# A graph layer on one Trainium2 core: gathering every 44th quad of edge tiles from SyncE instead of GpSimd

## The chip, the cores and the metric

The kernel runs on one core of a Trainium2 chip. A core has TensorE (PE, with its weight loads shown as PEld), VectorE (DVE), ScalarE (ACT), GpSimd (POOL) and SyncE (SP), which run side by side and wait for each other through semaphores, and 16 DMA engines that the queues of SP, ACT and POOL share. The metric is the device time of the whole program in microseconds (us), the median of several runs.

## What is computed

It is one equivariant graph layer with a residual and a layer norm. There are 12,500 nodes of 160 numbers (64 scalars, 32 vectors of three), and 400,000 edges, sorted by destination. Cut to what matters:

```
h     = linear(x) * a                           # per node: 64 + 96 numbers
w     = silu(edge_scalars @ fc_w1) @ fc_w2      # per edge: 224 weights
e     = h[edge_src]                             # the gather: 160 numbers per edge
m     = products of w, e and edge_attr          # per edge
agg   = segment_sum(m, edge_dst)                # per node
o     = linear(agg) + self_connection(x)
out   = layernorm(x + gated(o))
```

The row of `h` that an edge needs is given by `src`, which is random, so it has to be fetched by an index.

## The kernel before, in words

First the table `h_tab` (12,500 rows of 160 floats, 640 bytes each) is computed and written to DRAM (L245 to L315), and the destinations are reduced to the first node of every block (`rows`). Then the loop over the edges runs (L755 to L787), and it takes nearly the whole span.

A tile is 128 edges; 3125 tiles are taken four at a time, a quad, so there are 782 steps. Three tiles make a block, and 24 tiles (six steps) a chunk, whose edge scalars `es` are loaded together by two DMAs on SP (L219). The indices `idx` and the edge attributes `eat` are loaded for 60 tiles at a time (L180, L181). `fetch(n + 4)` asks for what the step four ahead needs.

In a step, these things happen:

- `gather` (L429): POOL issues four indirect DMAs, one per tile, which bring 128 rows of `h_tab` each into one of four `hg` buffers (pool `deep`). The gather for step n + 4 has to wait until DVE has done with the buffer in step n.
- `weights` (L438): PE multiplies the hidden layer `hid` with `w2` into `pw` (two PSUM buffers).
- `products` (L449): DVE multiplies `pw` and `hg` into `pr` in four instructions, one at L455 and three at L463. The last of them frees the `hg` buffer. Between them two hooks run, which may call `turn`'s second half (L571) and `add_up` (L727).
- `select_quad` (L495): DVE makes the selection matrix `sel` (L501, L504).
- `sum_up` (L712): PE multiplies `sel` of two steps earlier with `pr` and sums a block in `pa` (L511). A full pair of blocks is copied to SBUF by ACT (L677) and transposed by PE two steps later (L520).
- `hide(n + 2)` (L635): every other step PE and ACT compute the hidden layer (L424, L426) of the step two ahead.
- `output` (L691): once 16 blocks are ready, PE applies the second linear map (L536) and ACT copies the result to `os` (L539). The 16 results are added into `acc` by DVE (L544) at a base that comes from `rows`, two in a step at most, `add_up` handing them out.
- `finish` (L547): as soon as four tiles of nodes are complete, they are turned (PE, L570), gated, normed and stored (the `x` rows loaded at L564, the result stored at L603, both on SP). There are 25 such jobs. The last one has buffers of its own (pool `ends_fin`).

The order on PE, DVE, ACT and POOL in the loop is that of the program text (`manual_schedule`, L749); SP is not in that list there, and its order is chosen by the scheduler. Every DMA signals one of eight semaphores that the hardware queues take in turn (POOL has eight of its own), and an issue waits until the DMA before it on that semaphore has landed. The loop that repeats work for unusually wide blocks (L820 and on) is not entered with these inputs.

The bases of 16 blocks are read in one go in `output`, into 16 registers of DVE:

```
702:  _, values = nc.values_load_multi_w_load_instructions(
703:      rows[0:1, run[0]:run[0] + m], engines=[ENG.DVE], min_val=0, max_val=N - 1,
704:      skip_runtime_bounds_check_because="every entry of dst is the index of a node")
```

Of the kernel before, what the change touches and what calls it, by code (L numbers as in the profile page):

```python
# [10 lines left out]
F32 = mybir.dt.float32  # L11
I32 = mybir.dt.int32
I16 = mybir.dt.int16
BF16 = mybir.dt.bfloat16
# [17 lines left out]
Q = 4  # L32
SB = 4 * BT
SIDE = SB
AHEAD = 5 * SB
NF = 4

MARGIN = 128
NO = 16
# [13 lines left out]
def gnn_kernel(  # L53
# [21 lines left out]
    nc = tc.nc  # L75
    N = x.shape[0]
# [110 lines left out]
    def index(t):  # L187
        a0, idx, _ = ahead(t)
        return idx[:, t - a0:t - a0 + 1]
# [239 lines left out]
    def gather(pool, idx):  # L429
# [5 lines left out]
                in_offset=bass.IndirectOffsetOnAxis(ap=i, axis=0))  # L435
        return hg

    def weights(psum, hid, slots):  # L438

        pw = psum.tile([P, Q, 256], F32, name="pw")  # L440
        n = len(slots)
        for t in sorted(range(n), key=lambda t: (slots[t][1], slots[t][0])):
            half, c = slots[t]
            r = slice(half * S, (half + 1) * S)
            nc.tensor.matmul(pw[:, t, :NWT], hid[r, c * P:(c + 1) * P], w2[r],  # L445
                             start=True, stop=True)
        return pw
# [98 lines left out]

    def finish(fin, psum, t0, nt, p, most=NF):  # L547


        whole = nt if p == P else nt - 1  # L550
        xt = fin.tile([P, most, D], F32, name="xt")
        z = fin.tile([P, most, 2 * V3], F32, name="z")
        sg = fin.tile([P, most, V3], F32, name="sg")
        y = fin.tile([P, most, D], F32, name="y")
        st = fin.tile([P, most, 6], F32, name="st")
        mv = fin.tile([P, most, 2], F32, name="mv")
        rs = fin.tile([P, most], F32, name="rs")
# [8 lines left out]
        def turn(k):  # L566
            c = (t0 + k) * P
# [7 lines left out]
        def gates():  # L575
            nc.scalar.activation(sg[:, :nt], z[:, :nt, :V3], AF.Sigmoid)  # L576

        def gated():
            nc.vector.tensor_mul(y[:, :nt, :S], z[:, :nt, :S], sg[:, :nt, :S])
# [5 lines left out]
        def residual():  # L585
            nc.vector.tensor_add(y[:, :nt], y[:, :nt], xt[:, :nt])  # L586

        def moments():
            for k in range(nt):
# [4 lines left out]
        def root():  # L594
            nc.scalar.activation(rs[:, :nt], mv[:, :nt, 1], AF.Sqrt, bias=eps)  # L595

        def norm():
            nc.vector.reciprocal(rs[:, :nt], rs[:, :nt])
# [15 lines left out]

    with tc.tile_pool(
        name="fin", bufs=1
    ) as fin, tc.tile_pool(name="ends_fin", bufs=1) as ends_fin, tc.tile_pool(
        name="late", bufs=2
    ) as late, tc.tile_pool(name="edge", bufs=2) as edge, tc.tile_pool(
        name="deep", bufs=4  # L620
# [1 line left out]
        name="pa_ps", bufs=2, space=PSUM  # L622
    ) as pa_ps, tc.tile_pool(name="misc_ps", bufs=2, space=PSUM) as misc_ps:
        hids = {}

        def fetch(n):

# [63 lines left out]
        def output(n, blocks):  # L691
            while adds:
                for a in add_up(adds[0][0]):
                    add(*a)
            os = second(late, misc_ps, tts[0], tts[1], len(blocks))
            at_base = {}
            run = sorted(blocks)
            while run:
                m = 1
                while m < len(run) and run[m] == run[0] + m:  # L700
                    m += 1
                _, values = nc.values_load_multi_w_load_instructions(
                    rows[0:1, run[0]:run[0] + m], engines=[ENG.DVE], min_val=0, max_val=N - 1,
                    skip_runtime_bounds_check_because="every entry of dst is the index of a node")
                at_base.update(zip(run[:m], values))
                run = run[m:]
            adds.extend((n + 2, b, os, k, at_base[b]) for k, b in enumerate(blocks))

        assert NB % 2 == 0
        ended = set()  # L710
# [109 lines left out]
        with tc.For_i(0, n_redo, 1):  # L820
# [5 lines left out]
            with tc.For_i(0, n_again, 1) as g, tc.For_i(0, GT, 1) as k:  # L826
# [21 lines left out]
                with tc.For_i(first + W, last + 1, W) as base:  # L848
# [12 lines left out]
            for pool, job, most in [(fin, job, NF) for job in jobs] + [(ends_fin, last_job, LAST)]:  # L861
# [51 lines left out]
```

## Time and profile before

| what | value |
|---|---|
| median of 3 runs | 5161.72 us (5152.41 to 5164.67) |
| the profiled execution's own time | 5152.41 us |
| its span, first to last instruction | 5150.6 us |
| granted TensorE clock, mean | 0.829 |
| gathers on POOL (L433) | 3125, 966 ns each |
| packets of the gather queue | 150,000, 256.2 MB |
| packets of SP's queue | 128,802, 145.95 MB |
| mean DMA rate | 80 GB/s |

The time of a run is that of the program on the device, and the profile shows one such execution. In the views, a group's line gives the engine, the operation, the tiles written and read, the count, the busy time and the mean of one in nanoseconds, then the idle time of the engine just before and what ended most of it. In the waits, the three numbers are the total in us, how many times, and the longest. In the timeline, the first number is the start in us and the second the duration; what stands in brackets is the idle time before it and what ended it. "remote" is a semaphore whose sender the profile could not name; of the instruction at L455 it is PE's semaphore, the only one that instruction itself waits for.

### The profile page before, as it was taken

The page shows a single profiled execution, that of the slowest core. Times are in us where ns is not written, and L with a number is a line of the kernel's source. Part 1 is how long each engine was busy: PE and PEld are TensorE (multiplying, and loading weights), DVE is VectorE, ACT ScalarE, POOL GpSimd, SP SyncE. Part 2 cuts the span into 40 slices and gives each one's busy share as a digit, 9 for nine tenths or more (in the row PEclk, how much of TensorE's full clock was granted, in tenths as well). Part 3 has the DMA queues.
Part 4 walks back from the last instruction along what each step waited for, and adds up shares of the span by engine and source line. Part 5 has one row for each costly group of instructions (what it writes and reads, how often), then busy time and mean ns, then how long its engine had stood idle before and what let it go on. Part 6 is the DMA issues. An engine that isn't in the chain of part 4 may idle for free. (4 is left out here: it accounts for less than half of the span.)

```text
span 5150.6 us, 54423 instructions
## 1 busy us (share of the span) xinstructions
PE 3755.2 (73%) x17408; PEld 1766.8 (34%) x17408; DVE 2432.3 (47%) x6363; ACT 918.4 (18%) x3014; POOL 3040.2 (59%) x3134
## 2 busy tenths in 40 slices
PE   3776777766777777776777777777777777777776
PEld 3333333333333333333333333333333333333333
DVE  3444444544544444444444445444454444544545
ACT  0111111221211111111111122111121111211212
POOL 3665566656656556556566666665665565556554
PEclk7888888888888888887888888888887888888888
DMA  6333333333333333333333333333333333333322
GB/s 188 84 74 72 85 80 73 86 75 78 84 71 83 80 72 79 83 74 77 82 76 80 79 79 85 75 79 78 80 79 78 78 80 78 78 74 85 76 69 53
DMA packets 292619, 414.35 MB, mean 80 GB/s; under 512 B 74900, under 2 KB 239649, under 8 KB 292084
## 3 DMA queue, kind: packets, MB, share of 16 engines
q0 software_dynamic: 150000, 256.20, 20.6%
q1 hardware_dynamic: 128802, 145.95, 12.6%
q10 hardware_dynamic: 13526, 8.64, 0.6%
q8 instruction: 143, 2.34, 0.2%
q14 instruction: 148, 1.21, 0.1%
HBM read 394.54 MB, written 16.01 MB: 80 GB/s over the span
## 5 line engine op out<-in xcount | busy, mean ns | idle before, releaser
L433 POOL DMA_INDIRECT hg<-h_tab,idx x3125 | 3017.5, 966 | 2072.2 <-DVE oh L501 1113.3
L511 PE MATMUL pa<-pr,sel 128*64 128x416 f32 x6250 | 1599.8, 595 | 185.2 <-issue 160.5
L455 DVE TENSOR_TENSOR pr<-pw,hg 128x512 f32<-128x512 f32 x782 | 539.3, 690 | 2451.0 <-remote 1427.1
L445 PE MATMUL pw<-w,hid 64*128 64x224 f32 x6250 | 975.2, 419 | 363.8 <-issue 178.1
L463 DVE TENSOR_TENSOR pr<-pw,hg 128x384 f32<-128x384 f32 x2346 | 1154.0, 548 | 0.0
L445 PEld LDWEIGHTS pw<-w,hid 64*128 64x128 f32 x6250 | 629.0, 210 | 712.7 <-issue 508.3
L511 PEld LDWEIGHTS pa<-pr,sel 128*64 128x64 f32 x6250 | 456.4, 151 | 932.3 <-issue 867.9
L520 PE MATMUL pt<-ident,sa 128*128 128x128 f32 (+1 forms) x2084 | 378.1, 309 | 381.3 <-ACT hid L426 110.7
L677 ACT COPY sa<-pa 128x416 f32<-128x416 f32 x521 | 262.2, 503 | 1755.2 <-remote 706.0
L424 PE MATMUL ph<-es,w 128*128 128x512 f32 (+1 forms) x784 | 474.1, 686 | 54.3 <-ACT t L527 31.0
L520 PEld LDWEIGHTS pt<-ident,sa 128*128 128x128 f32 (+1 forms) x2084 | 238.2, 143 | 758.1 <-issue 392.5
L536 PE MATMUL po<-tt,l 128*96 128x256 f32 (+3 forms) x1360 | 346.8, 405 | 108.6 <-ACT t L527 67.3
L426 ACT ACTIVATE hid<-ph 128x512 f32<-128x512 f32 x392 | 233.7, 596 | 939.7 <-remote 516.8
L504 DVE TENSOR_TENSOR sel<-oh,eas 128x256 f32<-128x256 f32 x782 | 336.3, 430 | 37.5 <-ACT eas L488 0.2
L524 ACT COPY tt<-pt 128x192 f32<-128x192 f32 x521 | 165.3, 317 | 1027.3 <-remote 514.6
L536 PEld LDWEIGHTS po<-tt,l 128*96 128x96 f32 x1360 | 228.6, 178 | 243.0 <-issue 94.6
L424 PEld LDWEIGHTS ph<-es,w 128*128 128x128 f32 x784 | 128.2, 204 | 348.2 <-issue 268.2
L544 DVE TENSOR_TENSOR acc<-acc,os 96x32 f32 x1042 | 194.9, 187 | 26.3 <-ACT os L539 6.9
L501 DVE TENSOR_TENSOR oh<-rel,iota 128x64 f32<-128x64 int16 x782 | 171.4, 219 | 0.0
L570 PE MATMUL pp<-ident,acc 96*128 96x96 f32 x196 | 43.5, 313 | 171.8 <-DVE acc L544 98.0
L526 ACT COPY tt<-pt 128x32 f32<-128x32 f32 x521 | 103.0, 198 | 0.0
L539 ACT COPY os<-po 96x512 f32<-96x512 f32 (+2 forms) x68 | 38.3, 563 | 328.5 <-PE po L536 113.5
(70 smaller groups left out, 795.9 us busy)
## 6 DMA issues: line engine op xcount, KB each, us to landing
es<-in_es_t_dram SPq DMA_DIRECT2D x260, 384.0 KB
hg<-h_tab,idx POOLq DMA_INDIRECT x3125
h_tab<-ht ACTq DMA_DIRECT2D x6, 1280.0 KB
xt<-in_x_dram SPq DMA_DIRECT2D x23, 320.0 KB
out_dram<-y SPq DMA_DIRECT2D x23, 320.0 KB
xv<-in_xv_t_dram SPq DMA_DIRECT2D x25, 187.5 KB
eat<-in_ea_dram SPq DMA_DIRECT2D x30, 120.0 KB
xs<-in_xs_t_dram SPq DMA_DIRECT2D x25, 125.0 KB
```

The costliest lines, as they stand in the source:

```text
L424: nc.tensor.matmul(ph[:k, c], w1[:k, :k], es[:k, t0 * P + c0 * P:t0 * P + c1 * P], start=True, stop=True)
L426: nc.scalar.activation(hid[:k, c], ph[:k, c], AF.Silu, scale=1.0 / math.sqrt(64))
L433: nc.gpsimd.indirect_dma_start(out=hg[:, t, :], out_offset=None, in_=h_tab, in_offset=bass.IndirectOffsetOnAxis(ap=i, axis=0))
L445: nc.tensor.matmul(pw[:, t, :NWT], hid[r, c * P:(c + 1) * P], w2[r], start=True, stop=True)
L455: nc.vector.tensor_mul(two, pw[:, :n, :2 * S].rearrange("p t (k c) -> p t k c", k=2), hg[:, :n, None, :S].to_broadcast([P, n, 2, S]))
L463: nc.vector.tensor_mul(pr[:, :n, first:first + V3].rearrange("p t (i c) -> p t i c", i=3), pw[:, :n, None, 2 * S + k * V:2 * S + (k + 1) * ...
L504: nc.vector.tensor_mul(sel[:, :n], oh[:, :, None, :].to_broadcast([P, n, 4, W]), by_slot(tiles[0][0])[:, u:u + n, :, None].to_broadcast([P ...
L511: nc.tensor.matmul(pa[half * ROWS:(half + 1) * ROWS, :NPR], sel[:, t].rearrange("p k w -> p (k w)"), pr, start=start, stop=stop)
L520: nc.tensor.transpose(pt[:c, four * P:four * P + k], sa[:k, four * P:four * P + c], ident[:k, :k])
L536: nc.tensor.matmul(po[:, k, :nb], l2[:b, terms[to, part, four]], a[:, :nb], start=(n == 0), stop=(n == len(of) - 1))
L544: nc.vector.tensor_add(window, window, os[:, :, b])
L677: nc.scalar.copy(sa, pas.pop(j)[:, :NPR])
```

## The change

There are three edits.

1. Steps 52, 96, ..., 756 (every 44th, 17 in all; the list `own`) are not gathered by POOL. 50 steps ahead of such a step m, SP loads the 512 indices of the quad into `at_bytes` (four DMAs, `places`). 46 steps ahead DVE multiplies them by 640, to byte addresses, and 44 jobs are queued (`rows_of`). One job is issued in each step: SP reads 12 addresses (8 at the end of a tile) into registers and issues one plain DMA of 640 bytes per edge, from `h_tab` at that address to one partition of the buffer `hq` (two buffers). Step m then takes `hq` in the place of `hg`.
2. The last job of nodes uses the pool `fin` of the other jobs, with two buffers for `xt`; the other tiles are allocated when its first tile is turned (`held`). `ends_fin` is gone.
3. The base of a block is no longer read with 15 others in `output`, but alone in `add_up`, just before it is used, with the check of its bounds.

SP is added to the engines whose order in the loop is that of the program.

```diff
+OWN = 44
+BATCH = 12
...
+    own = [n for n in range(OWN + 8, len(steps) - 4, OWN) if len(steps[n][2]) == Q]
+    by_bytes = h_tab.rearrange("n d -> (n d)").bitcast(U8)
+    row_bytes = 4 * D
+    def places(pool, n):
+        at_bytes = pool.tile([Q, P], I32, name="at_bytes")
+        for k, (t, _, _) in enumerate(steps[n][2]):
+            g, u = divmod(t, GT)
+            with nc.allow_non_contiguous_dma(reason="the indices of one tile"):
+                nc.sync.dma_start(at_bytes[k:k + 1],
+                                  src[g][:, u:u + 1].rearrange("p u -> u p"))
+        return at_bytes
+    def rows_of(pool, at_bytes):
+        hq = pool.tile([P, Q, D], F32, name="hq")
+        flat_hq = hq.rearrange("p t d -> p (t d)").bitcast(U8)
+        jobs = []
+        for t, p0 in ((t, p0) for t in range(Q) for p0 in range(0, P, BATCH)):
+            def job(t=t, p0=p0):
+                _, values = nc.values_load_multi_w_load_instructions(
+                    at_bytes[t:t + 1, p0:min(P, p0 + BATCH)], engines=[ENG.SP], min_val=0,
+                    max_val=(N - 1) * row_bytes,
+                    skip_runtime_bounds_check_because="every entry of src is the index of a node")
+                for i, v in enumerate(values):
+                    p = p0 + i
+                    nc.sync.dma_start(flat_hq[p:p + 1, t * row_bytes:(t + 1) * row_bytes],
+                                      by_bytes[ds(v, row_bytes)][None])
+            jobs.append(job)
+        return hq, jobs
...
+        def fetch_rows(n):
+            for m in own:
+                if n == max(1, m - OWN - 6):
+                    at_of[m] = places(mine, m)
+                if n == max(3, m - OWN - 2):
+                    nc.vector.tensor_scalar_mul(at_of[m], at_of[m], float(row_bytes))
+                    hq_of[m], jobs = rows_of(mine, at_of[m])
+                    rows_due.extend((m, job) for job in jobs)
+            for _, job in rows_due[:1]:
+                job()
+            del rows_due[:1]
...
             fetch(n + 4)
-            hg = gather(deep, [index(t) for t, _, _ in tiles])
+            fetch_rows(n)
+            hg = hq_of.pop(n) if n in own else gather(deep, [index(t) for t, _, _ in tiles])
...
-        with tc.manual_schedule(engines={ENG.PE, ENG.DVE, ENG.Activation, ENG.Pool}):
+        with tc.manual_schedule(engines={ENG.PE, ENG.DVE, ENG.Activation, ENG.Pool, ENG.SP}):
...
-            at_base = {}
-            run = sorted(blocks)
-            while run:
...
-                _, values = nc.values_load_multi_w_load_instructions(
-                    rows[0:1, run[0]:run[0] + m], engines=[ENG.DVE], min_val=0, max_val=N - 1,
-                    skip_runtime_bounds_check_because="every entry of dst is the index of a node")
-                at_base.update(zip(run[:m], values))
-                run = run[m:]
-            adds.extend((n + 2, b, os, k, at_base[b]) for k, b in enumerate(blocks))
+            adds.extend((n + 2, b, os, k) for k, b in enumerate(blocks))
...
-            _, b, os, k, base = adds.pop(0)
+            _, b, os, k = adds.pop(0)
+            base = nc.values_load(rows[0:1, b:b + 1], engines=[ENG.DVE], min_val=0, max_val=N - 1)
...
-        xt = fin.tile([P, most, D], F32, name="xt")
+        xt = fin.tile([P, most, D], F32, name="xt", bufs=2)
+        held = []
...
-            last_steps = finish(ends_fin, misc_ps, *last_job, most=LAST)
+            last_steps = finish(fin, misc_ps, *last_job, most=LAST)
```

More of the change, by code (lines that the diff above doesn't have):

```diff
@@ L13 @@
 I16 = mybir.dt.int16
+U8 = mybir.dt.uint8
 BF16 = mybir.dt.bfloat16
@@ L550, in finish @@
         whole = nt if p == P else nt - 1
-        xt = fin.tile([P, most, D], F32, name="xt")
[L552 to L557, printed above, removed]
+        xt = fin.tile([P, most, D], F32, name="xt", bufs=2)
+        held = []
         if whole < nt:
@@ L566, in turn @@
         def turn(k):
+            if not held:
+                held.extend(fin.tile([P, most, *shape], F32, name=name) for name, shape in (
+                    ("z", [2 * V3]), ("sg", [V3]), ("y", [D]), ("st", [6]), ("mv", [2]),
+                    ("rs", [])))
+            z = held[0]
             c = (t0 + k) * P
@@ L575, in gates @@
         def gates():
+            z, sg = held[:2]
             nc.scalar.activation(sg[:, :nt], z[:, :nt, :V3], AF.Sigmoid)
         def gated():
+            z, sg, y = held[:3]
             nc.vector.tensor_mul(y[:, :nt, :S], z[:, :nt, :S], sg[:, :nt, :S])
@@ L585, in residual @@
         def residual():
+            y = held[2]
             nc.vector.tensor_add(y[:, :nt], y[:, :nt], xt[:, :nt])
         def moments():
+            _, _, y, st, mv, _ = held
             for k in range(nt):
@@ L594, in root @@
         def root():
+            mv, rs = held[4:]
             nc.scalar.activation(rs[:, :nt], mv[:, :nt, 1], AF.Sqrt, bias=eps)
         def norm():
+            _, _, y, _, mv, rs = held
             nc.vector.reciprocal(rs[:, :nt], rs[:, :nt])
@@ L616, in gnn_kernel @@
         name="fin", bufs=1
-    ) as fin, tc.tile_pool(name="ends_fin", bufs=1) as ends_fin, tc.tile_pool(
+    ) as fin, tc.tile_pool(
+        name="mine", bufs=2
+    ) as mine, tc.tile_pool(
         name="late", bufs=2
@@ L624, in gnn_kernel @@
         hids = {}
+        at_of, hq_of, rows_due = {}, {}, []
+        def fetch_rows(n):
[9 more added lines that the diff above has]
+            del rows_due[:1]
+            assert all(m > n for m, _ in rows_due)
         def fetch(n):
@@ L695, in output @@
             os = second(late, misc_ps, tts[0], tts[1], len(blocks))
-            at_base = {}
-            run = sorted(blocks)
-            while run:
-                m = 1
-                while m < len(run) and run[m] == run[0] + m:
-                    m += 1
-                _, values = nc.values_load_multi_w_load_instructions(
-                    rows[0:1, run[0]:run[0] + m], engines=[ENG.DVE], min_val=0, max_val=N - 1,
-                    skip_runtime_bounds_check_because="every entry of dst is the index of a node")
-                at_base.update(zip(run[:m], values))
-                run = run[m:]
-            adds.extend((n + 2, b, os, k, at_base[b]) for k, b in enumerate(blocks))
+            adds.extend((n + 2, b, os, k) for k, b in enumerate(blocks))
         assert NB % 2 == 0
@@ L860, in gnn_kernel @@
                     nc.vector.tensor_scalar_add(r, r, -float(W))
-            for pool, job, most in [(fin, job, NF) for job in jobs] + [(ends_fin, last_job, LAST)]:
+            for pool, job, most in [(fin, job, NF) for job in jobs] + [(fin, last_job, LAST)]:
                 job_steps = finish(pool, misc_ps, *job, most=most)
```

## The prediction, written before the result was known

> **What bounds the kernel now.** I read the page first, then the waits of DVE and POOL, then the timeline of those two engines, because the answer of the first two views is misleading here.
>
> ```profile
> PE 3755.2 (73%) x17408; PEld 1766.8 (34%) x17408; DVE 2432.3 (47%) x6363; ACT 918.4 (18%) x3014; POOL 3040.2 (59%) x3134
> ...
> L433 POOL DMA_INDIRECT hg<-h_tab,idx x3125 | 3017.5, 966 | 2072.2 <-DVE oh L501 1113.3
> ...
> L455 DVE TENSOR_TENSOR pr<-pw,hg 128x512 f32<-128x512 f32 x782 | 539.3, 690 | 2451.0 <-remote 1427.1
> ```
>
> No engine is full. POOL spends 966 ns in a gather and then 0.30 us of issue, so one gather per 1.25 us and a quad of four in 5.0 us; a step takes 6.43 us (the start of L455 in all 782 steps). POOL also stands idle 1113 us for a buffer that DVE has to free. The waits of DVE say the same from the other side:
>
> ```profile
> DVE pr L455 <- remote: 1427.1, 165, 14.5
> DVE pr L455 <- PE pw L445: 404.7, 145, 13.6
> ...
> DVE pr L455 <- DMA hg<-h_tab,idx: 86.3, 33, 4.4
> ```
>
> DVE waits for PE's semaphore, hardly for a gather. By the packets of the gather queue a quad has landed 8 us or more before L455 uses it in all but four of the 782 steps. Read so far, the gathers have slack and taking some off POOL gains nothing. The timeline of POOL and DVE speaks against that reading. First POOL, then DVE, over one such wait:
>
> ```profile
> 2618.20 0.95 POOL L433 DMA_INDIRECT hg<-h_tab,idx  x1 [0.31 <-issue]
> 2619.45 0.95 POOL L433 DMA_INDIRECT hg<-h_tab,idx  x1 [0.30 <-issue]
> 2625.96 1.14 POOL L433 DMA_INDIRECT hg<-h_tab,idx  x1 [5.56 <-DVE oh L501]
> ```
>
> ```profile
> 2606.42 0.69 DVE L455 TENSOR_TENSOR pr<-pw,hg 128x512 f32<-128x512 f32 x1
> 2607.02 1.48 DVE L463 TENSOR_TENSOR pr<-pw,hg 128x384 f32<-128x384 f32 x3
> ...
> 2623.61 0.69 DVE L455 TENSOR_TENSOR pr<-pw,hg 128x512 f32<-128x512 f32 x1 [14.52 <-remote]
> ```
>
> POOL gathers without a pause from 2600.5 to 2620.4 us, and runs out of its four buffers. 3.2 us later PE's answer arrives and DVE goes on, after 14.5 us of idleness; 2.35 us later (L455 and three L463) POOL has a buffer again. I counted this over the trace: POOL's gathers form 258 uninterrupted runs of 15.1 us on average with 4.4 us of idleness between them, and from the end of a run to the next L455 it is 2.7 us, the middle half between 2.2 and 3.1 us; for the 99 runs of 16 gathers it is 2.9 to 3.1 us in the middle half. If PE's lateness had nothing to do with POOL, this interval would be scattered. So PE's results become visible late while POOL issues gathers, and come in a burst about 3 us after it stops. Why, the trace does not tell (the ends of matmuls are modelled). But the idle time of POOL is then no slack: a cycle is a run of gathers, 5.0 us per quad, plus a fixed 4.4 us. That adds up: 258 x (15.1 + 4.4) = 5030 us of the 5150.6 us span. POOL's gathers set the time.
>
> **The change, part by part.**
>
> *17 quads leave POOL.* `own` starts at step 52, goes by 44 and ends before step 778: 52, 96, ..., 756, all of four tiles. POOL loses 68 of 3125 gathers: 68 x 1.25 us = 85 us if the number of pauses stays; 17 x 6.43 = 109 us if the pauses go with them, since the four hg buffers then reach over five steps where one of them is an own one. I take the middle, -97 us.
>
> *SP gets 512 plain DMAs per own quad*, as 44 jobs, one in each step: read up to 12 byte addresses into registers, issue 12 DMAs of 640 bytes. No row shows a DMA at a register's address. Below: the three one-descriptor DMAs of SP (L334, L337, L339) took 242, 251 and 223 ns and stood 0.29 us apart. Above: the 607 ns of an es load (four by 64 pieces). I take 0.29 to 0.33 us, the row with the same shape. The register read has rows on DVE (L702, 16 values 1.10 us, two values 0.54), so some 0.94 us for 12. A job is then 12 x 0.31 + 0.94 = 4.7 us, and at the upper end 12 x 0.61 + 0.94 = 8.3 us. SP's own work is about 0.4 us a step (481 DMAs in the loop, 235 us); DMAs share eight semaphores in turn, so after each pair of es loads, which lands 5.1 us after issue, SP stands some 3 us once in six steps, 0.5 us a step. Sum 5.6 us of the 6.43 us of a step: it fits, with 0.8 us to spare, and breaks at 0.38 us per DMA.
>
> SP is now also kept in the order of the program. Behind a waiting SP instruction stand the es, idx and eat loads. The store of y waits for DVE (L603, 223 us in 16 waits, longest 45.2), so SP has no lead at those 25 places, and once per own quad for the multiplication of the indices. From there an es load is issued two steps, 13 us, before PE needs it, and lands in 5.1 us plus at most one job: just enough. Cover gone, it costs a few microseconds at some of 42 places: 0 to 60 us, I take 10, since today es is issued 36 us or more ahead of its first matmul in 19 of 20 chunks. The idx loads come late by at most a job, under the 8 us that a landed quad waits. HBM bytes stay; a quad's 512 descriptors replace 512 rows of a gather.
>
> The row here is the es pair: SP issues the second 0.65 us after the first while the data land after 5.1 us, so DMAs overlap and a small one costs its issue. The Trainium skill (DMA: Bandwidth & Descriptors, "Rules for kernel authors") says the opposite of this change: coalesce many small transfers, since below 64 KB one pays mostly overhead; its section on the anatomy of a DMA puts the fixed part at about 2.0 us. Paid one after another, 8704 x 2.0 us would be 17 ms, an estimate from that page; with eight in flight 2.2 ms, which would fit beside the 5.1 ms. I go by the row.
>
> *DVE reads each base alone.* Before: 68 reads of 16 registers (L702, 1.10 us), beside L504 and behind the L463 that frees POOL's buffer, so their going gains little (0 to 68 x 0.7 = 48 us; I take 0, what is late next is PE). After: 1042 reads, up to two in a step, the first behind L455, the second behind the first L463. One read took 309 ns on DVE and 477 ns on SP (L819); with a bounds check SP added 180 and 33 ns. So 0.31 to 0.69 us, against the 0.60 us from L455 to L463 and 0.47 us from one L463 to the next that hide them: 0 to 0.3 us come through in a step that has two, some 8 of 12. It counts where POOL waits for that L463, in the 258 pauses: 258 x 2/3 x 0.17 = 30 us, between 0 and 258 x 2/3 x 0.5 = 86 us. Elsewhere the delay lies beside POOL's run. The 17 multiplications of 4x128 indices, at most 0.4 us each, are under 7 us, put at 0.
>
> *The last job shares buffers.* In the trace the job before it stores y at 5111.4 us, and the last one writes y at 5136.6: the buffer is free 20 us earlier. It costs 0, at most the 2 us of a landing. xt gets a second buffer, off the path.
>
> Sum: -97 + 10 + 30 + 2 = -55 us. The profiled execution took 5152.4 us (span 5150.6, 1.8 around it), so 5097 there; it is the fastest of three, 9.3 us below their median, so on the median of 5161.7 the forecast is 5106 us. I write **5105**. Its own range: -109 with nothing lost gives 5053, -85 with 75 lost gives 5152; 5050 to 5150.
>
> **Rivals.** A difference of 0.3%, 15 us, is about what a measurement of this kernel can tell from no change.
>
> *POOL's pauses are slack and PE is the bound* (no gain): for it speak DVE's waits, which name PE, 73% of PE's span and a landed quad that waits 8 us. Against it the fixed 3 us after a run's end. Then only the costs remain, 0 to 42 us: 5160 to 5200, around 5170. Chance 0.18.
>
> *SP becomes the bound* (slower): its place is the job of each step, its price the time of one DMA, and it decides from 0.38 us on. At 0.40 us a step takes 12 x 0.40 + 0.94 + 0.9 = 6.6 us, 748 steps 160 us more: 5320; at 0.45 us it would be 5760. For it: no row shows an address from a register, and es issues take 607 ns. Against: one-descriptor issues of 223 to 251 ns. Chance 0.14.
>
> *DVE's single reads eat the gain*: 86 us and late es loads against 85 to 109: 5150 to 5200. Chance 0.08.
>
> *The change doesn't do what it says*: SP holds PE's or POOL's answer back as POOL does, so that the own quads relieve nothing and the 12 DMAs in every step add to the lateness: above 5200. Chance 0.04 inside the slower ones, beyond the others.
>
> The forecast keeps 0.56. Faster by over 0.3%: 0.56 and the good ends of the first and third rivals, 0.60 in all. Within: 0.17. Slower: 0.23. For 8 in 10 I leave out what lies below 5045 and SP as the bound: 5045 to 5200.
>
> **What the profile after would show.** Right: 3057 indirect gathers at L433's successor, still 1.25 us apart; fewer pauses or the same, each 4.4 to 4.7 us; around an own step a run of gathers that spans five steps; SP's DMAs of 640 bytes at 0.29 to 0.33 us; no wait of L455 on hq; DVE reads of 0.3 to 0.7 us behind L455. Wrong, if POOL's busy time falls by 66 us (68 x 966 ns) and its idle time grows by as much (PE is the bound), if PE's hidden-layer matmul (L424) waits for es (SP is late), or if the time from L455 to POOL's next gather grows from 2.35 us by more than 0.3 us.

## Result and profile after

The changed kernel takes 6411.59 us (median of 4 runs, 6392.49 to 6420.74) against 5163.06 us for the kernel before on the same chip (4 runs): 1.242 times as long, 95% interval [1.2385, 1.2453]. The forecast was 5105 us. The profiled execution took 6407.27 us, its span is 6405.4 us, and the mean granted TensorE clock fell from 0.829 to 0.766 of full speed.

Lines of kernel.py have moved: the gather L433 is now L436, the first product L455 is L490, the other three L463 are L498, the hidden layer L424 is L427, the weights L445 are L480, `oh` L501 is L536. The new edge DMAs are L468, the read of 12 addresses L462. First the page of the changed kernel, busy time by engine and the groups that answer to those of before:

```profile
PE 3792.0 (59%) x17408; PEld 1806.6 (28%) x17408; DVE 2519.6 (39%) x6380; ACT 926.9 (14%) x3014; POOL 2966.6 (46%) x3066
...
L436 POOL DMA_INDIRECT hg<-h_tab,idx x3057 | 2943.9, 963 | 3386.5 <-DVE oh L536 1848.9
L490 DVE TENSOR_TENSOR pr<-pw,hg 128x512 f32<-128x512 f32 x765 | 527.7, 690 | 3470.2 <-remote 1371.0
...
L427 PE MATMUL ph<-es,w 128*128 128x512 f32 (+1 forms) x784 | 564.8, 805 | 1619.2 <-DMA es<-in_es_t_dram 1504.8
```

POOL issues 68 gathers fewer, 963 ns each as before, and its busy time falls by 74 us; but its idle time grows from 2072 to 3386 us. New in the list is the last line: PE's hidden layer stands 1505 us for `es`, the edge scalars that SP loads. The waits of all engines say the same; the columns are us in total, times, longest:

```profile
POOL hg L436 <- DVE oh L536: 1848.9, 275, 29.8
...
PE ph L427 <- DMA es<-in_es_t_dram: 1504.8, 114, 40.8
DVE pr L490 <- remote: 1397.5, 137, 33.3
DVE pr L490 <- PE pw L480: 1359.7, 218, 36.8
...
POOL hg L436 <- DMA hq<-h_tab: 315.0, 24, 24.9
...
POOL hg L436 <- DMA idx<-in_src_dram: 202.0, 12, 30.1
```

Read it from PE outwards: `es` is late, so the hidden layer is late, so `pw` and the product are late, and POOL's buffers come free late. No engine of this chain is full. SP is, and the waits hide it, because issuing a DMA does not count as busy: all of SP's waits together are some 420 us of 6405. The loads of `es` and `idx` stand behind the edge DMAs in SP's order.

Why SP is full shows in its timeline. A line gives start, length, and how many issues were put together. SP while POOL is in the middle of a run of gathers:

```profile
3003.57 12.05 SPq L468 DMA_DIRECT2D hq<-h_tab  x7
```

and once that run is over:

```profile
3019.16 4.99 SPq L468 DMA_DIRECT2D hq<-h_tab  x11
```

Seven edges in 12.05 us, with one read of addresses among them, then eleven in 4.99 us, again with one read. One level deeper, the two instructions that an edge on SP consists of, a register MOVE and the DMA itself (count, then shortest, median and longest in ns, then the stretch in us), inside the run:

```profile
L468 SPq MOVE hq<-h_tab x5: 3/698/702, 3007.1 to 3014.2; - x5
L468 SPq DMA_DIRECT2D hq<-h_tab x5: 688/712/720, 3007.1 to 3014.9; - x5
```

and after it:

```profile
L468 SPq MOVE hq<-h_tab x15: 2/29/707, 3018.4 to 3024.8; - x15
L468 SPq DMA_DIRECT2D hq<-h_tab x15: 3/228/262, 3019.1 to 3024.9; - x15
```

POOL in the same stretch gathers until 3016.1 us and then has to wait 9.19 us for a buffer:

```profile
3015.18 0.95 POOL L436 DMA_INDIRECT hg<-h_tab,idx  x1 [0.30 <-issue]
3025.32 0.94 POOL L436 DMA_INDIRECT hg<-h_tab,idx  x1 [9.19 <-DVE oh L536]
```

The busy times of the engines in two stretches, one inside the run and one in the pause:

```profile
3003.00:3015.00 12.00, 6.29 (x27) 2.44 (x23) 0.00 (x0) 1.22 (x9) 9.13 (x10) 0.86 0.28 69
3019.00:3025.00 6.00, 4.76 (x14) 1.98 (x15) 5.34 (x13) 1.85 (x6) 0.00 (x0) 0.50 0.01 3
```

(columns: length, busy PE, PEld, DVE, ACT, POOL with their instructions, granted clock, DMA share, GB/s.) DVE does nothing in the 12 us in which POOL gathers and 5.34 of 6 us in the pause; the 16 DMA engines are 28% busy, so they are not what is full. Nor does a low clock hold the work back in the run: it is granted at 0.86 there and at 0.50 in the pause.

Counted over the whole trace by the age of POOL's run, the median time from one edge to the next is 0.32 us while POOL is idle and in the first 2 us of a run, 0.44 us from 2 to 4 us, 1.10 us from 4 to 6 us, 0.74 us from 6 to 8 us, and 1.43 us from 8 us on (the means grow steadily: 0.50, 0.58, 0.98, 1.06 and 1.62 us over the five stretches of a run). From 6 us on the median time from the start of one of the two instructions to the start of the next is about 0.7 us, for the MOVE as for the DMA. Of the 8703 intervals between edges 5410 are under 0.45 us and make up 1598 us; 1620 lie between 1.2 and 2.5 us and make up 2550 us. A step takes 6405 / 782 = 8.2 us.

### The profile page after: what moved, and what is told of

It is laid out like the page before. It is cut to its first block, busy times and chain, and to the rows that moved or that the text cites. A ratio compares the mean times of both kernels' runs of the same rounds, so it can differ in the third digit from the quotient of the medians.

```text
span 6405.4 us, 75666 instructions
## 1 busy us (share of the span) xinstructions
PE 3792.0 (59%) x17408; PEld 1806.6 (28%) x17408; DVE 2519.6 (39%) x6380; ACT 926.9 (14%) x3014; POOL 2966.6 (46%) x3066
## 5 line engine op out<-in xcount | busy, mean ns | idle before, releaser
L436 POOL DMA_INDIRECT hg<-h_tab,idx x3057 | 2943.9, 963 | 3386.5 <-DVE oh L536 1848.9
L490 DVE TENSOR_TENSOR pr<-pw,hg 128x512 f32<-128x512 f32 x765 | 527.7, 690 | 3470.2 <-remote 1371.0
L546 PE MATMUL pa<-pr,sel 128*64 128x416 f32 x6250 | 1515.4, 585 | 154.2 <-issue 132.0
L427 PE MATMUL ph<-es,w 128*128 128x512 f32 (+1 forms) x784 | 564.8, 805 | 1619.2 <-DMA es<-in_es_t_dram 1504.8
L498 DVE TENSOR_TENSOR pr<-pw,hg 128x384 f32<-128x384 f32 x2295 | 1176.6, 551 | 85.4 <-issue 22.9
L480 PE MATMUL pw<-w,hid 64*128 64x224 f32 x6250 | 964.7, 426 | 230.4 <-DVE oh L536 109.2
L480 PEld LDWEIGHTS pw<-w,hid 64*128 64x128 f32 x6250 | 633.6, 215 | 604.7 <-issue 466.9
L427 PEld LDWEIGHTS ph<-es,w 128*128 128x128 f32 x784 | 145.4, 229 | 1906.1 <-issue 1821.2
L546 PEld LDWEIGHTS pa<-pr,sel 128*64 128x64 f32 x6250 | 436.1, 151 | 845.5 <-issue 777.8
L571 PE MATMUL po<-tt,l 128*96 128x256 f32 (+3 forms) x1360 | 395.0, 449 | 8.9 <-DVE z L606 6.5
L571 PEld LDWEIGHTS po<-tt,l 128*96 128x96 f32 x1360 | 268.2, 205 | 189.9 <-issue 90.8
L536 DVE TENSOR_TENSOR oh<-rel,iota 128x64 f32<-128x64 int16 x782 | 170.1, 218 | 0.0
```

Source lines behind the costliest of these rows:

```text
L427: nc.tensor.matmul(ph[:k, c], w1[:k, :k], es[:k, t0 * P + c0 * P:t0 * P + c1 * P], start=True, stop=True)
L436: nc.gpsimd.indirect_dma_start(out=hg[:, t, :], out_offset=None, in_=h_tab, in_offset=bass.IndirectOffsetOnAxis(ap=i, axis=0))
L490: nc.vector.tensor_mul(two, pw[:, :n, :2 * S].rearrange("p t (k c) -> p t k c", k=2), hg[:, :n, None, :S].to_broadcast([P, n, 2, S]))
L498: nc.vector.tensor_mul(pr[:, :n, first:first + V3].rearrange("p t (i c) -> p t i c", i=3), pw[:, :n, None, 2 * S + k * V:2 * S + (k + 1) * ...
L546: nc.tensor.matmul(pa[half * ROWS:(half + 1) * ROWS, :NPR], sel[:, t].rearrange("p k w -> p (k w)"), pr, start=start, stop=stop)
L571: nc.tensor.matmul(po[:, k, :nb], l2[:b, terms[to, part, four]], a[:, :nb], start=(n == 0), stop=(n == len(of) - 1))
```

## Experiments

All ratios are to the kernel before, run on the same chip. "Gap" below is the time from one edge DMA to the next.

**Everything but SP's edges** (changed kernel; 17 quads use rows that POOL gathered once):

```
-            for m in own:
+            if n == 0:
+                still.append(gather(mine, [index(t) for t, _, _ in steps[0][2]], "still"))
+            if n in own:
+                hq_of[n] = still[0]
+            for m in ():
```

> The changed kernel without SP's part: no indices loaded, no jobs, no 640-byte DMAs. The 17 own steps take one quad of rows that POOL gathered at the start, so the gather of those quads is left out; program order of SP, single reads of the bases and the shared buffers stay. Theory now (SP's queue is the bound, nothing else of the change costs much): the 24% go altogether and the first step of the prediction shows alone, 5163 less 85 to 109 plus up to 40: 5050 to 5110. Rival 'PE is the bound and POOL's pauses are slack': 5150 to 5200. Rival 'the program order of SP makes the loads late' or 'the reads on DVE': still above 6000.

Measured: 1.0026 [1.0001, 1.0052]. So what costs 24% is SP's edge work alone; all other parts of the change add up to nothing. (Its first gather waits for the space of its extra buffer: the first product starts at 128.7 us instead of 97.8, so some of the gain is lost at the start.) The ratio is not the gain that the theory named; it lies where the rival 'PE is the bound' had it. Two later runs tell why that is no support for this rival: the 17 quads do save time (0.9900 below), and the single reads cost as much again (1.0099, next but one).

**SP in program order** (kernel before):

```
-        with tc.manual_schedule(engines={ENG.PE, ENG.DVE, ENG.Activation, ENG.Pool}):
+        with tc.manual_schedule(engines={ENG.PE, ENG.DVE, ENG.Activation, ENG.Pool, ENG.SP}):
```

> The kernel before, with SP kept in program order in the loop and nothing else. Theory now: SP has next to nothing to do, so the order costs 0 to 20 us: 5155 to 5185. Rival 'the order makes the loads late': the larger part of the 1250 us, above 5700.

Measured: 1.0006 [0.9986, 1.0026]. The order by itself costs nothing that can be measured; it only makes the loads late when something slow stands ahead of them.

**Single reads of the bases** (kernel before):

```
...
-            _, b, os, k, base = adds.pop(0)
+            _, b, os, k = adds.pop(0)
+            base = nc.values_load(rows[0:1, b:b + 1], engines=[ENG.DVE], min_val=0, max_val=N - 1)
```

> The kernel before, with each base read alone on DVE, with its bounds checked, just before its use, and nothing else. Prediction's step: +30 us, between 0 and 86, so 5163 to 5250, around 5190. Rival 'the reads carry much of the loss': above 5400.

Measured: 1.0099 [1.0064, 1.0135], 51 us. A read takes 301 ns on DVE (the median of 1042). At the pauses of POOL the time from the first product to the next gather grows from 2.47 to 2.66 us on the mean; 257 pauses by 0.19 us are 49 us, which accounts for all of it.

**Half as many quads on SP** (changed kernel):

```
-OWN = 44
+OWN = 88
...
-            for _, job in rows_due[:1]:
-                job()
-            del rows_due[:1]
+            if n % 2 == 0:
+                for _, job in rows_due[:1]:
+                    job()
+                del rows_due[:1]
```

> The changed kernel with every 88th quad (8 quads instead of 17) and one job of 12 edges in every second step, so that SP has two steps for each. Theory now: a threshold. A job took 8.2 us of SP on average against steps of 6.43 us; with 12.9 us for it SP is no longer the bound and the loss goes nearly altogether: 5080 to 5250. Rival 'each DMA on SP costs the other engines something, in proportion': half of the 1250 us stays, 5750 to 5850.

Measured: 1.0306 [1.0284, 1.0328]. PE's wait for `es` falls from 1505 us to 2.7 us: SP is no longer the bound, and 21 of the 24% are gone, so most of the loss is a threshold, as the theory had it, and not a half of 24%. The 3% that stay are above the theory's range all the same. They are more than the single reads cost: 1.0306 less 0.0099 for them, plus some 0.005 for eight quads spared, leaves about 0.025, 130 us for 4096 edges or 32 ns each, which must be paid outside SP's queue.

**The loads of es, idx and eat issued by ACT** (changed kernel):

```
-                nc.sync.dma_start(to[:, :n * P], es_t[:, e0:e0 + n * P])
+                nc.scalar.dma_start(to[:, :n * P], es_t[:, e0:e0 + n * P])
```

and the same in three further places.

> The changed kernel with the loads of es, idx and eat issued by ACT, so that nothing PE needs stands behind the edges in SP's order. Theory now (SP's own pace is the bound: 44 jobs for 44 steps): DVE waits for hq in the place of PE for es, the time stays between 5900 and 6450. Rival 'only the loads stuck behind the jobs cost time': it falls to 5200 to 5450.

Measured: 7127.49 us, 1.3987 [1.3937, 1.4037]; both expectations missed. PE's waits name what is late instead, the loads of `xs` that stayed on SP:

```profile
PE psc L715 <- DMA xs<-in_xs_t_dram: 1238.1, 24, 86.1
PE pw L480 <- DVE oh L536: 809.3, 61, 79.7
```

The wait for `es` has gone (18 us are left of 1505), but whatever still stands behind the edges is late. SP also waits 856 us before an edge DMA for an `es` load to land (99 us before): SP and ACT take the same eight semaphores in turn, so an edge on SP now waits for a load that ACT issued. Moving the loads away treats the symptom.

**Few gathers** (kernel before; POOL gathers three quads, which all later steps use) **and the edges alone** (the changed kernel, cut in the same way, its own quads still from SP):

```
-        name="deep", bufs=4
+        name="deep", bufs=1
...
-                hg = gather(deep, [index(t) for t, _, _ in tiles])
+                if n < 3:
+                    still.append(gather(deep, [index(t) for t, _, _ in tiles], f"still{n}"))
+                hg = still[n % 3]
```

> The kernel before with POOL gathering for the first three steps only; all later steps take those three quads of rows again, so nearly all of the gather is left out. Theory 'POOL's gathers hold back PE's answers': PE answers at once, a step takes about DVE's 3.2 us to 4 us, 2600 to 3500 in all. Rival 'PE is the bound and POOL's pauses are slack': the time stays within 5% of before, above 4850.

> The changed kernel with the same cut: POOL gathers for the first three steps only, the own steps still get their rows from SP. Theory 'POOL's gathers also slow SP's instructions': the edges come 0.32 us apart throughout, a job takes 4.9 us and with the rest of SP's work 5.7 us, so SP is the bound at 4200 to 4700. Rival 'SP is slow by itself': the mean distance stays near 0.70 us and the time near 6400.

Measured: 3217.65 us and 4493.01 us, one execution each. Without gathers the kernel before is 37% shorter, so POOL's gathers do set the time. PE becomes the bound only then:

```profile
PE 3098.1 (96%) x17408; PEld 1545.5 (48%) x17408; DVE 2405.3 (75%) x6363; ACT 934.2 (29%) x3014; POOL 34.2 (1%) x21
```

With the edges alone, 7689 of 8703 gaps are under 0.45 us (median 0.32) and a step takes 4491 / 782 = 5.7 us; PE waits 985 us for `es`. That is SP as the bound at its quiet price, and it is close to the prediction's 5.6 us a step. The same SP work takes 8.2 us a step beside the gathers.

**17 quads not gathered** (kernel before, with the last job in shared buffers; 17 quads use rows gathered once):

```
-                hg = gather(deep, [index(t) for t, _, _ in tiles])
+                if n == 0:
+                    still = gather(spare, [index(t) for t, _, _ in tiles], "still")
+                hg = still if n in own else gather(deep, [index(t) for t, _, _ in tiles])
...
-            last_steps = finish(ends_fin, misc_ps, *last_job, most=LAST)
+            last_steps = finish(fin, misc_ps, *last_job, most=LAST)
```

> The kernel before, with batched reads, where the 17 own steps take one quad of rows gathered at the start (their gather is left out, SP gets nothing). The gain of the change alone. Prediction's step: 85 to 109 us, ratio 0.979 to 0.984. From the two runs so far, no edges against single reads: 1.0026 less 0.0099, ratio 0.990 to 0.995. Rival 'no gain at all': 1.000.

Measured: 0.9900 [0.9876, 0.9924], 51 us less. The extra buffer delays the first product from 97.8 to 132.3 us, of which 14 us are still there at the sixth step; with 14 to 34 us added back the 17 quads are worth 65 to 85 us.

**A fixed address in each edge DMA** (changed kernel; the own quads get other rows):

```
-                for i, v in enumerate(values):
-                    p = p0 + i
+                for p in range(p0, min(P, p0 + BATCH)):
+                    v = (t * P + p) * 37 % N * row_bytes
...
-                                      by_bytes[ds(v, row_bytes)][None])
+                                      by_bytes[v:v + row_bytes][None])
```

> The changed kernel, but each of SyncE's 8704 edge DMAs has a fixed address in place of one from a register, so the register MOVE ahead of each is gone (the reads of 12 addresses stay, their values unused; the rows of the own quads are other rows than the indices name). Theory now: beside POOL's gathers SP is held at every instruction, about 0.7 us each whatever it is, so half as many instructions halve the price of an edge: mean pitch 0.35 to 0.42 us instead of 0.70, a step needs some 6 us of SP, SP is no longer alone in setting the time: 5300 to 5600 us. Rival A, the DMA itself is what is held and the MOVE only shows the wait: mean pitch stays 0.65 to 0.70 us, 6100 to 6420 us. Rival B, the address from a register is what costs: pitch 0.23 to 0.30 us also beside gathers, 5150 to 5350 us.

Measured: 1.0399 [1.0376, 1.0423], 5308 us. The MOVE is gone, and the median gap is 0.29 us with POOL idle (0.32 before) but 0.71 us from 8 us of a run on (1.43 before). The number of instructions counts: one costs about 0.7 us there, two cost twice that. The mean gap of 0.57 us lies in none of the three ranges named; it also contains time in which SP waits for other engines. The time lies within both the theory's range and that of rival B, so it doesn't tell them apart; the gaps beside gathers do, since rival B would have them at 0.23 to 0.30 us.

**Plain DMAs on POOL** (changed kernel, the lookup left out), and later **the same on the kernel before**:

```
-            nc.gpsimd.indirect_dma_start(
-                out=hg[:, t, :], out_offset=None, in_=h_tab,
-                in_offset=bass.IndirectOffsetOnAxis(ap=i, axis=0))
+            nc.gpsimd.dma_start(out=hg[:, t, :], in_=h_tab[t * P:(t + 1) * P, :])
```

> The changed kernel, but POOL's 3057 gathers are plain DMAs of 128 consecutive rows of the table, of the same 128 x 640 bytes to the same tiles (the lookup by index is left out). Theory now: it is the descriptors that POOL makes for an indirect DMA, or the reading of indices, that holds the other engines' sequencers; with plain DMAs SP's mean pitch falls to 0.33 to 0.45 us and the time to 4600 to 5500 us. Rival, any DMA that POOL issues, or the 82 KB of small rows that each moves, holds them as much: mean pitch 0.6 us or more, 6000 us or more.

> The kernel before, but POOL's 3125 gathers are plain DMAs of 128 consecutive rows of the table (the lookup by index is left out; the same bytes to the same tiles). Theory now: it is the indirect form, not the bytes, that holds the other engines; without it the kernel ends near the run that leaves nearly all gathers out (3218 us): 3200 to 3500 us. Rival, the transfers themselves are part of it: 4000 us or more.

Measured: 0.8952 [0.8927, 0.8977], 4569.87 us, on the changed kernel, and 0.6236 [0.6212, 0.6259], 3218.40 us, on the kernel before. In the first, 7644 of 8703 gaps are under 0.45 us although POOL brings in the same bytes, so SP isn't held; the mean gap of 0.49 us, just above the theory's range, is that of the run with hardly any gathers (0.48). It isn't only that plain DMAs come in shorter runs: over 4 us into a run of plain DMAs lie 399 edges (27 if a rest of 0.5 us, and not of 1 us, ends a run), and their median gap is still 0.32 us. The second ends where the run with few gathers ended, 3218 us. From its page, engines and the group on POOL:

```profile
PE 3100.6 (96%) x17408; PEld 1548.0 (48%) x17408; DVE 2417.2 (75%) x6363; ACT 934.3 (29%) x3014; POOL 1677.8 (52%) x3134
...
L433 POOL DMA_DIRECT2D hg<-h_tab x3125 | 1655.1, 536 | 1497.8 <-DVE oh L499 1328.8
```

The queue that carries them is the same in both kernels, with the same 150000 packets and 256.20 MB. The bytes, the packets and the landing in `hg` cost nothing that shows beside a PE that is 96% busy; leaving out the indirect form takes the kernel from 5158 to 3218 us. Of these 1940 us some 790 are POOL's own pace: 3125 indirect gathers 1.25 us apart and 100 us at the start are 4010 us, whatever the others do. The other 1150 us or so are POOL's pauses (1113 us of waits for DVE in the kernel before), the share that a hold on the other engines can account for. The plain DMAs always read the same 512 rows of the table, so the random places and the reading of the indices go out together with the indirect form; the runs don't separate the three. PE also gets a higher clock in the plain run (0.98 against 0.83), and how much of the 1940 us that makes was not taken apart.

**Four quads on SP, bases read 16 at a time** (changed kernel: OWN = 176, a job in every fourth step, the batched reads put back):

> The changed kernel with only 4 quads on SyncE (each 176th, a job of 12 edges in every fourth step) and with the bases read 16 at a time as in the kernel before. Theory now, by the half-as-many run: each edge DMA costs the others about 29 ns, 2048 of them 59 us, and 4 quads spare POOL 12 us: 1.007 to 1.011 times the kernel before. Rival, the loss there came of bursts of SP work beside other loads and is no price per DMA; then so thin a stream costs nothing and the spared quads show: 0.996 to 0.999.

Measured: 1.0125 [1.0098, 1.0152], a little above the theory's range and far from the rival's. So this thin stream doesn't pay either: 1.5% against the 0.9976 that four spared quads would give, 77 us for 2048 edges, 37 ns each. With the half-as-many run (32 ns) and the fixed address (1.0399 less 1.0026, 190 us for 8704, 22 ns) that is a price per edge beside the time on SP itself. It is what is left over after the other terms, not a thing seen in a trace, and how it comes about is open.

**Three buffers for gathered quads** (kernel before, `bufs=4` to `bufs=3`):

> The kernel before with 3 buffers for gathered quads instead of 4, so that POOL's runs of gathers get shorter. If it is the length of a run that holds PE's answers back (in the changed kernel SP was quick for the first 2 us of a run and slow after 4 us), runs of 10 to 11 us instead of 15.1 hold them less: 0.95 to 0.995. Rival, POOL loses lead and waits for a free buffer more, and what is held is held in proportion to the number of gathers: 1.00 to 1.06.

Measured: 0.9990 [0.9973, 1.0007]. POOL's runs did not get shorter (15.1 us), so this tells nothing on their length, only that the fourth buffer isn't needed here.

**A pause on POOL after each quad**, first in the changed kernel, then in the kernel before (nothing is left out in these and the next three):

```
+        pause = pool.tile([P, 128], F32, name="pause", bufs=1)
+        for _ in range(8):
+            nc.gpsimd.memset(pause, 0.0)
```

> The changed kernel with a pause of about 1.6 us on POOL after each quad of gathers (eight small fills of a scratch tile), so that no run of gathers is longer than 5 us. Theory now: SP is quick in the first 2 us of a run and held from about 4 us on, so runs of 5 us leave it nearly free: mean pitch of an edge 0.35 to 0.50 us, SP no longer sets the time alone, 5250 to 5700 us. Rival, what is held goes with the number of gathers and not with the length of a run: pitch stays 0.6 us or more, 6300 to 7000 us.

> The kernel before with the same pause after each quad. By the theory that a run holds PE's answers only once it is long, the pauses take the place of the waits that POOL has anyway (1113 us for DVE): 782 steps of 5.0 us of gathers and 1.6 us of pause are 5160 us, with the start 5200 to 5300 us. Rival, the held answers do not come sooner and the 1250 us of pauses come on top: 5700 to 6400 us.

Measured: 1.1158 [1.1116, 1.1200] and 1.1354 [1.1321, 1.1387]. The eight fills take 2.1 us and the gap between quads becomes 2.6 us, 1 us more than planned, so a quad takes 7.35 us; 782 x 7.35 + 100 = 5850 us is what the second shows (5859.81). POOL waits for nobody any more, neither in the changed kernel

```profile
POOL hg L436 <- issue: 1168.4, 2997, 69.2
POOL hg L436 <- DVE pr L493: 24.2, 46, 0.6
```

nor in the kernel before

```profile
POOL hg L433 <- issue: 1182.4, 3082, 66.9
POOL hg L433 <- DVE pr L458: 20.1, 40, 0.5
```

where it waited 1113 us for DVE without the pauses ("issue" is its own 0.3 us ahead of each gather). So the theory for the kernel before was right that the waits go and wrong on the time, which lies in the rival's range for the longer pause alone. The changed kernel's time lies between the ranges of theory and rival, and its mean gap, 0.62 us, is the rival's (0.6 or more). On SP the median gap from 4 to 6 us of a run is now 0.70 us (1.10 without pauses), there is no later part of a run, and the mean contains waits for other engines; PE waits only 16 us for `es`. And the changed kernel got faster by being given 765 pauses: 5759 against 6411 us. On the same chip it is now 0.983 of the kernel before with pauses, 101 us less: 17 quads of 7.35 us are 125 us. With POOL full and SP no longer the bound, the change saves about what the quads it spares POOL are worth, which is the gain that the forecast had counted on.

**Shorter pauses**: 4 fills and 2 fills in the kernel before, 4 fills in the changed kernel.

> The kernel before with 4 fills after each quad instead of 8: a quad then takes POOL 6.3 us (with 8 fills 7.35 us from one quad's start to the next, and POOL waited for no other engine). If short runs keep the other engines free, POOL again waits for nearly nothing: 782 x 6.3 us and 100 us at the start, 4950 to 5080 us, 0.96 to 0.985 of the kernel before. Rival, what is held needs the longer pause to come free and POOL's waits come back: 5150 to 5500 us.

> The kernel before with 2 fills after each quad: 5.8 us for a quad if POOL doesn't wait. If the pauses may be as short as that: 4600 to 4750 us. If the held answers need some 1.2 us or more in 6 to come through, POOL waits for DVE again and the time is near that of the kernel before: 4900 to 5200 us, which is what the theory now expects, since SP was held from 4 us on in a run and 5.8 us leave too short a rest.

> The changed kernel with 4 fills after each quad: 765 x 6.3 us and 100 us on POOL are 4920 us, but SP needs 12 edges at 0.55 to 0.62 us and an own share of some 1.5 us in each step, 7.1 to 8 us when it is held as in the run with 8 fills: 5500 to 6200 us, SP the bound again. Rival, the shorter step has the same share of rest and SP is no worse off than POOL: 4900 to 5300 us.

Measured: 0.9797 [0.9762, 0.9832], 5067 us; 0.9536 [0.9500, 0.9571], 4934 us; 1.0228 [1.0192, 1.0265], 5291 us. The first two lie in the ranges that the theory named. The kernel before with two fills after each quad beats both kernels, by 4.6% and 23%. POOL's timeline in it, a quad in 5.7 us:

```profile
3001.36 0.96 POOL L433 DMA_INDIRECT hg<-h_tab,idx  x1 [0.50 <-issue]
3002.62 0.94 POOL L433 DMA_INDIRECT hg<-h_tab,idx  x1 [0.30 <-issue]
3003.87 0.95 POOL L433 DMA_INDIRECT hg<-h_tab,idx  x1 [0.30 <-issue]
3005.12 0.95 POOL L433 DMA_INDIRECT hg<-h_tab,idx  x1 [0.30 <-issue]
3006.07 0.49 POOL L438 MEMSET pause<- 128x128 f32 x2
3007.06 1.08 POOL L433 DMA_INDIRECT hg<-h_tab,idx  x1 [0.50 <-DVE pr L466]
```

and its waits:

```profile
POOL hg L433 <- issue: 1103.6, 2931, 69.2
POOL hg L433 <- DVE oh L504: 366.3, 144, 13.7
```

A gap of 1 us after each quad, in place of 0.3 us, takes away two thirds of POOL's wait for DVE (1113 to 366 us), for 335 us of fills; with four fills the wait is 22.5 us. The changed kernel with four fills came out lower than the theory had it, inside the rival's range, and still waits 1539 us for `es`: SP remains its bound, and against the kernel before with the same four fills (0.9797) the change still loses 4.4%.

## Why the prediction was wrong, point by point

- **SP's price of an edge is the step that failed**: "I take 0.29 to 0.33 us, the row with the same shape", and "it fits, with 0.8 us to spare, and breaks at 0.38 us per DMA". The rows were those of L334, L337 and L339, which run 68 to 71 us into the span, before POOL's first gather at 90 us (and only the first two stood 0.29 us apart; the third came 2.27 us later). The price is right for that state (0.32 us measured, 1.00 us for a read of 12 addresses against 0.94 taken; 5.7 us a step with the edges alone). Beside a run of gathers an edge costs 1.43 us from 8 us on, and over all edges 0.70 us on the mean, other SP work included: 8.2 us a step where 6.43 were to be had. So the second rival came true, with its place and its threshold but not for the reason it gave (an address from a register costs a MOVE of 29 ns when POOL is quiet), and it was given 0.14. A smaller slip beside it: the 235 us named for SP's own DMAs are 0.30 us a step, not 0.4.
- **The reading that would have warned was in the prediction**: PE's results become visible late while POOL gathers. It was taken as something between POOL and PE. The fourth rival (SP "holds PE's or POOL's answer back") had the hold running in the wrong direction: it is POOL's indirect gathers that hold SP, and by the runs with plain DMAs and with pauses the other engines' progress too.
- **POOL's gathers set the time**: right. 3218 us without them, and with eight fills the time is POOL's own sum. In the changed kernel it is SP that sets it.
- **17 quads at -97 us**: 51 us measured, 65 to 85 us without the late start of that run, so at or below the low end of "85 us if the number of pauses stays". It nearly did: 250 waits for DVE against 257.
- **Program order at +10 us**: nothing (0.9986 to 1.0026). **Single reads at +30 us, up to 86**: +51 us, by the longer way from the first product to the next gather, as described. **Shared buffers**: not seen in the sum of the run without edges, 1.0026.
- **What the profile after would show**: 3057 gathers 1.25 us apart, true; POOL's busy time fell by 74 us (68 gathers are 66 us), but its idle time grew by 1314 us and not by as much, so the sign named for PE as the bound was not given. Not foreseen: POOL's pauses over 1 us are 319 in the place of 257 and 7.8 us long on the mean, not 4.4 to 4.7, and L490 does wait for `hq` (86.8 us in 9 waits). The sign named for a late SP, the hidden-layer matmul waiting for `es`, is the largest new wait of the profile; the sign for late reads, over 0.3 us more from the product to the next gather, is just met in the median (2.35 to 2.68 us).
- The issue of a DMA is not always as small as the Trainium skill has it: "DMA: Bandwidth & Descriptors", section "Issuing engines are not separate DMA queues", says that issuing from several engines at once saves only sequencer time, usually little beside the transfer. Here sequencer time, 0.32 to 1.43 us an edge, is what made SP the bound. The same page ("SWDGE vs HWDGE vs iDMA") puts plain and indirect DMAs of GpSimd on the same software path; the trace agrees for the queue (150000 packets on the software queue in both), but not for the cost beside it, 3218 against 5158 us. The 2.0 us that the prediction takes from the same page stands there, in the section "Anatomy of one DMA — SWDGE (gpsimd) path", for DMAs that GpSimd issues, while the edges go from SP; the sum didn't use it.

What stays open: what in the indirect form, or in the random rows and indices that go with it, holds the other engines. It takes some 4 us of a run to begin, it isn't that the DMA engines are full (28% busy inside a run), it isn't the number of bytes or packets, and it goes by the instruction on SP (0.7 us, DMA or MOVE). Every execution on record carries the profiler's span and clock; none without the profiler is there to show that an instruction is held for the same time when nothing is recorded. The runs show no more than that.

## What to carry to other kernels

Price an operation that you move to another engine from rows in which the engine you relieve is at work, since here the row from a quiet stretch was only a lower bound; a queue that is planned 87% full has no room for the difference. An engine that only issues DMAs shows no busy time: find it by its instructions per step times their pitch, and by who waits for the loads behind it. Where answers come late while one engine is in a long burst, try short pauses in that burst before moving work off it: here two small fills per quad gave 4.6%.

## What was not expected of the hardware

- Beside an uninterrupted run of indirect gathers on GpSimd, SyncE's instructions for an edge start about 0.7 us apart (median, from 6 us of the run on), a register MOVE (29 ns long otherwise) like a DMA of 640 bytes (228 ns otherwise).
- The same bytes in the same packets, brought by plain GpSimd DMAs (536 ns each, not 963), hold nobody so that it shows: 3218 us, as with hardly any gathers (3218 us), though always from the same 512 rows.
- Pauses in GpSimd's gathers let the other engines catch up: 1 us after each quad, 0.9536 of the time of the kernel before; in the changed kernel 2.6 us after each quad, 5759 instead of 6411 us.
- Each edge DMA costs some 22 to 37 ns beside its time on SyncE, even where SyncE is far from full (a remainder of three runs, not seen directly).
